# Decoder megakernel, last feed-forward: accumulators copied out by ScalarE, roots in pieces, norm on ScalarE

## The chip, the cores and the metric

The kernel runs on one core of a Trainium2 chip, in one launch. The metric is the device time of the launch in microseconds (us). The run before has three timed executions and, apart from them, one profiled execution, from which all durations below come.

## The reference

Two decoder layers run over x (4 batches, 512 positions, 512 features), each as attention, cross attention and feed-forward, each with a residual and a layer norm behind it. The change concerns the last of the six parts alone:

```python
def _L1_ffn_ref(x, gate_up_packed, gate_up_scales, down_packed, down_scales):
    ...
    gate_up = jnp.einsum('bsh,oh->bso', x, w_gu)      # weights from 4-bit codes, 11 blocks of 128 rows
    gate, up = (gate_up[..., :I], gate_up[..., I:])
    h = jax.nn.silu(gate) * up
    y = jnp.einsum('bsi,hi->bsh', h, w_down)
    rms = jnp.sqrt(jnp.mean(y * y, axis=-1, keepdims=True) + EPS)   # EPS = 1e-06
    return y / rms
...
x = _layernorm(x + _L1_ffn_ref(x, ...), axis=-1)      # mean and variance over 512, eps 1e-05
return x
```

## The kernel before

**Batches and lanes.** The six parts are called A to F, and a batch of a part is a task (F0 to F3 are the last feed-forward). Each task is a Python generator that issues instructions and yields; two tasks are live at a time and take turns. A task that yields "next" lets the following one start. So when F0 has issued its last up-projection it yields "next", and its ending is issued in turn with the beginning of F1. A `Pipe` delays a step by a number of ticks (`F_SCALED` 1, `F_ACT` 5, `F_PAIR` 3, `F_DOWN` 9). From what is issued, a scheduler settles the order on each engine; each engine then works its own queue strictly in that order and waits on semaphores.

**One batch of F.** x is loaded as four tiles of 128 positions (names `x`), transposed (`fx`) and split into a high and a low part. For each of 11 blocks i, for u = 0 (gate) and 1 (up), and for each of four groups g of 128 features, two matmuls fill a PSUM bank named `fg` (L1080). `scaled` takes the bank out: for g = 0 ScalarE multiplies by the group's scale (L1038); else VectorE multiplies and adds to the sum in SBUF (L1044, one scalar_tensor_tensor); for u = 0, g = 3 ScalarE makes a second tile (L1041) that GpSimd adds (L1048). Then Silu on ScalarE (L1052), gate times up on VectorE (L1056), the high part as a cast on ScalarE (`fhh`, L1061) and the low part on GpSimd (`fhl`, L1062). `down` issues three matmuls for each of the four position tiles t into four accumulators `facc` (L1071), which hold four of the eight PSUM banks through all 11 blocks. In all a batch has 176 matmuls into `fg` and 132 into `facc`.

**The ending of a batch.** It follows the "next": x is loaded again; ScalarE squares each accumulator and sums the row (L1090); VectorE makes the mean square (L1093) and its inverse root with an integer seed and three Newton steps (`rsqrt`, L158 to L163, 128x4 values); L1097 on VectorE adds accumulator times root to x, reading the accumulator in PSUM, and `ln_stats` takes bn_stats and bn_aggr of the sum (L168, L169). `finish` runs a second root (L177, then L158 to L163), the norm on VectorE (L186) and the stores from the SP queue (L189). The accumulators' banks are free when L1097 has read them.

Of the kernel before, what the change touches and what calls it, by code (L numbers as in the profile page):

```python
# [14 lines left out]
I32 = mybir.dt.int32  # L15
U8 = mybir.dt.uint8
AF = mybir.ActivationFunctionType
ALU = mybir.AluOpType
# [4 lines left out]
P = 128  # L23
NT = 4
MAGIC = 12582912.0
RSQRT_SEED = float(0x5F3759DF)
# [38 lines left out]
class Net:  # L65
# [88 lines left out]
    def rsqrt(self, ve, s):  # L154

        nc = self.nc
        sh, y, t = s[:, 0:4], s[:, 4:8], s[:, 8:12]
        nc.vector.tensor_scalar(sh.bitcast(I32), ve.bitcast(I32), 1, None, ALU.logical_shift_right)  # L158
        nc.vector.tensor_scalar(y.bitcast(I32), sh.bitcast(I32), -1.0, RSQRT_SEED, ALU.mult, ALU.add)
        for _ in range(3):  # L160
            nc.vector.tensor_tensor(t, y, y, ALU.mult)
            nc.vector.scalar_tensor_tensor(t, t, -0.5, ve, ALU.mult, ALU.mult)
            nc.vector.scalar_tensor_tensor(y, t, 1.5, y, ALU.add, ALU.mult)  # L163
        return y

    def ln_stats(self, y, i, ln):
        nc = self.nc
        nc.vector.bn_stats(ln[:, 8:14], y)  # L168
        nc.vector.bn_aggr(ln[:, 2 * i : 2 * i + 2], ln[:, 8:14])  # L169
# [852 lines left out]
    def l1_ffn(self, b):  # L1022
        nc = self.nc
        pipe = Pipe()
        x = self.load_x(5, b)
        yield
        yield
        xT = []
        yield from self.feature_major(pipe, x, "fx", xT)
        yield from pipe.drain()  # L1030
        acc, y, hs = [], {}, {}

        def scaled(i, u, g, ps):

            s = self.gs[:, (i * 2 + u) * 4 + g : (i * 2 + u) * 4 + g + 1]
            if g == 0:
                y[u] = self.t("fg")
                nc.scalar.activation(y[u], ps, AF.Copy, scale=s)  # L1038
            elif g == 3 and u == 0:
                y2 = self.t("fg2")  # L1040
                nc.scalar.activation(y2, ps, AF.Copy, scale=s)  # L1041
                y[u, 2] = y2
            else:
                nc.vector.scalar_tensor_tensor(y[u], ps, s, y[u], ALU.mult, ALU.add)  # L1044
            if g == 3:
                o = y.pop(u)
                if (u, 2) in y:
                    nc.gpsimd.tensor_tensor(o, o, y.pop((u, 2)), ALU.add)  # L1048
                pipe.later(F_ACT, *((up, i, o) if u else (gate, o)))

        def gate(o):
            nc.scalar.activation(o, o, AF.Silu)  # L1052
            y["gate"] = o

        def up(i, o):
            nc.vector.tensor_tensor(o, o, y.pop("gate"), ALU.mult)  # L1056
            pipe.later(F_PAIR, pair, i, o)

        def pair(i, o):
            hi, lo = self.t("fhh", F32R), self.t("fhl", F32R)  # L1060
            nc.scalar.copy(hi, o)  # L1061
            nc.gpsimd.tensor_tensor(lo, o, hi.bitcast(F32), ALU.subtract)  # L1062
            for t in range(NT):
                pipe.later(F_DOWN + 2 * t, down, i, t, (hi, lo))

        def down(i, t, h):
            if len(acc) <= t:
                acc.append(self.pb("facc"))
            c = slice(t * P, (t + 1) * P)
            for n, (l, r) in enumerate(((0, 0), (0, 1), (1, 0))):  # L1070
                nc.tensor.matmul(acc[t], h[l][:, c], self.dn[i][r], start=i == 0 and n == 0, stop=i == 10 and n == 2)  # L1071

        for i in range(11):
            self.need("F", lambda: len(self.dn) > min(10, i + 1))
            for u in range(2):
                for g in range(4):
                    pipe.tick()
                    ps = self.pa("fg")
                    for n in range(2):
                        nc.tensor.matmul(ps, self.gu[i, u][:, g * P : (g + 1) * P], xT[g][n], start=n == 0, stop=n == 1)  # L1080
                    pipe.later(F_SCALED, scaled, i, u, g, ps)
                    yield
        yield "next"
        x = self.load_x(5, b)
        yield from pipe.drain()
        fm = self.s("fm", 24, 2)
        ss, ve = fm[:, 0:4], fm[:, 4:8]
        for i in range(NT):
            sq = self.t("fsq")
            nc.scalar.activation(sq, acc[i], AF.Square, accum_out=ss[:, i : i + 1])  # L1090
            if i % 2:
                yield
        nc.vector.tensor_scalar(ve, ss, 1.0 / 512.0, 1e-6, ALU.mult, ALU.add)  # L1093
        r = self.rsqrt(ve, fm[:, 8:20])
        ln = self.ln_tile()
        for i in range(NT):
            nc.vector.scalar_tensor_tensor(x[i], acc[i], r[:, i : i + 1], x[i], ALU.mult, ALU.add)  # L1097
            self.ln_stats(x[i], i, ln)
            if i % 2:
                yield  # L1100
        self.finish(pipe, x, ln, 5, b)
        yield from pipe.drain()

    def need(self, key, ready):

# [121 lines left out]
```

## Time and profile before

| | us |
|---|---|
| median of three runs | 1662.6 (1662.27 to 1663.54) |
| profiled execution | 1662.88 |
| its span, first to last instruction | 1660.9 |
| mean granted TensorE clock | 0.978 of full |

| engine | busy us | share of the span |
|---|---|---|
| TensorE matmul (PE) | 1549.7 | 93% |
| VectorE (DVE) | 1267.4 | 76% |
| ScalarE (ACT) | 1007.5 | 61% |
| GpSimd (POOL) | 667.4 | 40% |

| instruction of F | count | mean ns |
|---|---|---|
| L1044 VectorE scaled sum | 220 | 745 |
| L1038 ScalarE scaled first sum | 88 | 686 |
| L1090 ScalarE square of an accumulator, and its readback | 16 | 594, 201 |
| L1097 VectorE update of x | 16 | 738 |
| L1048 GpSimd add | 44 | 1387 |
| L1062 GpSimd low part | 44 | 1317 |

In rows of the profile "L1044 DVE" is line 1044 on VectorE, "fg<-fg,gs,fg" the tiles written and read, and "[1.92 <-DVE fg L1044]" an idle time of the engine before that instruction, in us, and what ended it. Busy time of matmuls counts overlapping instructions once; a busy TensorE can still be slowed, which the granted clock shows.

### The profile page before, as it was taken

How to read it: one execution, taken by the hardware profiler on the slowest of the kernel's cores; microseconds unless marked ns; L12 is line 12 of the kernel's file. 1: busy time of each engine (PE TensorE's matmuls, PEld its weight loads, DVE VectorE, ACT ScalarE, POOL GpSimd, SP SyncE). 2: the span in 40 equal slices, each digit the busy share in tenths (PEclk: the TensorE clock that was granted, in tenths of full speed). 3: DMA queues.
4: the chain of work that ended last, by engine and by line, in shares of the span. 5: the costliest groups of instructions: out<-in, count | busy, mean ns of one | idle time of the engine just before them, and what ended most of it. 6: DMA issues, size and time to landing. Idle time of an engine off the chain costs nothing.

```text
span 1660.9 us, 25661 instructions
## 1 busy us (share of the span) xinstructions
PE 1549.7 (93%) x8246; PEld 1110.3 (67%) x8246; DVE 1267.4 (76%) x2796; ACT 1007.5 (61%) x2149; POOL 667.4 (40%) x672
## 2 busy tenths in 40 slices
PE   7999999999999899899999999999988889999995
PEld 5888775444544674466777767777667766786874
DVE  6386688999976678876565675756879999979795
ACT  5333326888778867786696865968533445444542
POOL 5663653555535203420435332343323344333332
PEclk9999998999999999999999999999998999999998
DMA  7043343455114634763433323333444532021000
GB/s 243 28 146 121 127 133 118 144 165 184 58 71 146 193 114 138 205 188 98 127 77 77 77 64 109 83 77 77 153 152 123 189 106 63 9 69 47 5 26 25
DMA packets 103237, 180.77 MB, mean 109 GB/s; under 512 B 16560, under 2 KB 18608, under 8 KB 103104
## 3 DMA queue, kind: packets, MB, share of 16 engines
q1 hardware_dynamic: 98976, 170.69, 32.8%
q0 software_dynamic: 4128, 8.46, 2.1%
q8 instruction: 65, 1.06, 0.3%
q14 instruction: 68, 0.56, 0.1%
HBM read 111.98 MB, written 41.94 MB: 93 GB/s over the span
## 4 chain that ended last, share of the span: by engine, by line
PE 54%; DVE 23%; ACT 9%; DMA 7%; issue 4%; POOL 2%; SPq 1%; DVEq 0%; ACTq 0%; POOLq 0%
PE fg L1080 7%; PE facc L1071 6%; DVE bsm L413 3%; PE dT L857 2%; ACT de L847 2%; PE pu L626 2%; PE pg L624 2%; DVE x L186 2%; DMA z<-had_scratch 2%; DVE fg L1044 2%; PE dn L678 2%; PE dq L146 2%; PE dq L147 2%; PE dq L148 2%; PE do L877 2%
## 5 line engine op out<-in xcount | busy, mean ns | idle before, releaser
L1044 DVE SCALAR_TENSOR_TENSOR fg<-fg,gs,fg 128x512 f32<-128x512 f32 x220 | 162.4, 745 | 36.8 <-PE fg L1080 17.5
L1080 PE MATMUL fg<-fxh,gu 128*128 128x512 f32 x352 | 144.2, 410 | 7.5 <-DVE fg L1044 4.6
L847 ACT ACTIVATE de<-de,dm 128x128 f32<-128x128 f32 (+3 forms) x256 | 143.0, 563 | 13.4 <-DVE dm L846 12.4
L846 DVE CUSTOM_DVE_ANT_0 de<-ds,negm,thr 128x128 f32<-128x128 f32 (+3 forms) x256 | 126.5, 546 | 31.0 <-PE ds L835 27.9
L421 POOL TENSOR_SCALAR be<-be,bsm 128x512 f32<-128x512 f32 x128 | 95.7, 760 | 120.5 <-DVE bsm L419 70.4
L1080 PE MATMUL fg<-fxl,gu 128*128 128x512 f32 x352 | 139.2, 395 | 0.0
L603 POOL TENSOR_TENSOR hl<-g,hh 128x512 fp32r<-128x512 f32 x64 | 84.2, 1323 | 114.6 <-ACT hh L602 93.4
L1048 POOL TENSOR_TENSOR fg<-fg,fg 128x512 f32<-128x512 f32 x44 | 61.0, 1387 | 128.4 <-ACT fg L1041 69.5
L415 ACT ACTIVATE be<-bs,bsm 128x512 f32<-128x512 f32 x128 | 87.5, 690 | 39.3 <-DVE bsm L413 32.3
L777 POOL TENSOR_TENSOR dql<-dqf,dqh 128x512 fp32r<-128x512 f32 x32 | 41.4, 1295 | 154.5 <-ACT dqh L776 120.8
L857 PE MATMUL dT<-ident,de 128*128 128x128 f32 x640 | 89.9, 278 | 7.9 <-ACT de L847 5.9
L1080 PEld LDWEIGHTS fg<-fxh,gu 128*128 128x128 f32 x352 | 67.3, 191 | 38.1 <-DVE fg L1044 14.2
L857 PEld LDWEIGHTS dT<-ident,de 128*128 128x128 f32 x640 | 71.7, 141 | 25.6 <-ACT de L847 14.4
L1038 ACT ACTIVATE fg<-fg,gs 128x512 f32<-128x512 f32 x88 | 60.4, 686 | 39.1 <-PE fg L1080 38.6
L413 DVE TENSOR_REDUCE bsm<-bs 128x1 f32<-128x512 f32 x128 | 84.0, 674 | 0.1
L692 PE MATMUL had<-had,z 128*128 128x128 f32 x512 | 75.0, 293 | 9.5 <-DMA z<-had_scratch 9.3
L692 PEld LDWEIGHTS had<-had,z 128*128 128x128 f32 x512 | 68.9, 203 | 17.1 <-issue 6.4
L1071 PE MATMUL facc<-p4h,fhh 128*128 128x512 f32 x176 | 71.7, 409 | 8.9 <-DVE fg L1044 6.2
L437 PE MATMUL bo<-bpT,cT 128*64 128x512 f32 x256 | 75.4, 625 | 3.5 <-ACT bpT L428 1.5
L199 PEld LDWEIGHTS bT<-ident,be 128*128 128x128 f32 x512 | 55.1, 141 | 34.4 <-issue 12.9
L199 PE MATMUL bT<-ident,be 128*128 128x128 f32 x512 | 73.7, 283 | 3.9 <-POOL be L421 1.4
L1041 ACT ACTIVATE fg<-fg,gs 128x512 f32<-128x512 f32 x44 | 30.2, 687 | 75.1 <-PE fg L1080 75.1
(330 smaller groups left out, 4715.8 us busy)
## 6 DMA issues: line engine op xcount, KB each, us to landing
x<-x SPq DMA_DIRECT2D x176, 256.0 KB, 3.1
had_scratch<-hw SPq DMA_DIRECT2D x64, 256.0 KB, 2.0
z<-had_scratch SPq DMA_DIRECT2D x64, 256.0 KB, 6.6
stk<-dqh SPq DMA_DIRECT2D x192, 64.0 KB, 2.1
tw<-in_wg_t SPq DMA_DIRECT2D x32, 256.0 KB, 4.1
tw<-in_wu_t SPq DMA_DIRECT2D x32, 256.0 KB, 3.5
tw<-in_wd_t SPq DMA_DIRECT2D x32, 256.0 KB, 2.7
p<-in_gu_p SPq DMA_DIRECT2D x22, 256.0 KB, 2.7
```

The source lines that it names most:

```text
L199: self.nc.tensor.transpose(pt[:, i * P : (i + 1) * P], srcs[i][:, j * P : (j + 1) * P], self.ident)
L413: nc.vector.tensor_reduce(sm[:, h : h + 1], ps, AX.X, ALU.max, negate=True)
L415: nc.scalar.activation(e, ps, AF.Exp, bias=sm[:, h : h + 1], accum_out=sm[:, 2 + h : 3 + h])
L421: nc.gpsimd.tensor_scalar(es[h][i], es[h][i], sm[:, 4 + h : 5 + h], 1.0, ALU.mult, ALU.mult)
L603: nc.gpsimd.tensor_tensor(lo, g, hi.bitcast(F32), ALU.subtract)
L692: nc.tensor.matmul(ps[:, c * P : (c + 1) * P], z[g * 4 + c][:, i * P : (i + 1) * P], self.had16, start=True, stop=True)
L846: nc.vector.tensor_tensor_reduce(es[i], ps, self.negm[:, 384 - P * i :], -1.0, self.thr[:, i : i + 1], ALU.add, ALU.min, n4[:, i : i + 1])
L847: nc.scalar.activation(es[i], es[i], AF.Exp, bias=n4[:, i : i + 1], scale=-1.0, accum_out=den[:, hh * 4 + i : hh * 4 + i + 1])
L857: nc.tensor.transpose(pt[:, o + (i - j) * P : o + (i - j + 1) * P], es[i][:, j * P : (j + 1) * P], self.ident)
L1044: nc.vector.scalar_tensor_tensor(y[u], ps, s, y[u], ALU.mult, ALU.add)
L1071: nc.tensor.matmul(acc[t], h[l][:, c], self.dn[i][r], start=i == 0 and n == 0, stop=i == 10 and n == 2)
L1080: nc.tensor.matmul(ps, self.gu[i, u][:, g * P : (g + 1) * P], xT[g][n], start=n == 0, stop=n == 1)
```

## The change

At the end of a batch of F, four ScalarE copies take the accumulators from PSUM to SBUF tiles `fy`, each as its accumulator closes; squares and the update of x read `fy`. The root is issued in pieces by a generator, `rsqrt_spread`, which yields before each Newton step; `issue_after(self.summed.ins)` puts each piece on VectorE's queue behind the latest scaled sum issued so far, of whichever batch. The update of x also writes its row sum (`accum_out`). GpSimd makes the negative mean from it (128x1), ScalarE squares x less its mean and sums the row, VectorE makes the second root, GpSimd mean times root (128x4), and ScalarE applies the norm and issues the store from its own queue. bn_stats, bn_aggr, VectorE's norm and SP's stores of this part are gone. The order on all engines is unchanged up to the first ending of F.

```diff
             else:
-                nc.vector.scalar_tensor_tensor(y[u], ps, s, y[u], ALU.mult, ALU.add)
+                self.summed = nc.vector.scalar_tensor_tensor(y[u], ps, s, y[u], ALU.mult, ALU.add)
...
+    def newton(self, ve, y, t):
+        nc = self.nc
+        nc.vector.tensor_tensor(t, y, y, ALU.mult)
+        nc.vector.scalar_tensor_tensor(t, t, -0.5, ve, ALU.mult, ALU.mult)
+        nc.vector.scalar_tensor_tensor(y, t, 1.5, y, ALU.add, ALU.mult)
+
+    def rsqrt_spread(self, ve, s):
+        nc = self.nc
+        sh, y, t = s[:, 0:4], s[:, 4:8], s[:, 8:12]
+        with self.tc.issue_after(self.summed.ins):
+            nc.vector.tensor_scalar(sh.bitcast(I32), ve.bitcast(I32), 1, None, ALU.logical_shift_right)
+            nc.vector.tensor_scalar(y.bitcast(I32), sh.bitcast(I32), -1.0, RSQRT_SEED, ALU.mult, ALU.add)
+        for _ in range(3):
+            yield
+            with self.tc.issue_after(self.summed.ins):
+                self.newton(ve, y, t)
...
+        ys = [self.o("fy") for i in range(NT)]
+        for i in range(NT):
+            nc.scalar.copy(ys[i], acc[i])
         for i in range(NT):
             sq = self.t("fsq")
-            nc.scalar.activation(sq, acc[i], AF.Square, accum_out=ss[:, i : i + 1])
+            nc.scalar.activation(sq, ys[i], AF.Square, accum_out=ss[:, i : i + 1])
             if i % 2:
                 yield
         nc.vector.tensor_scalar(ve, ss, 1.0 / 512.0, 1e-6, ALU.mult, ALU.add)
-        r = self.rsqrt(ve, fm[:, 8:20])
+        yield from self.rsqrt_spread(ve, fm[:, 8:20])
+        r = fm[:, 12:16]
         ln = self.ln_tile()
-        for i in range(NT):
-            nc.vector.scalar_tensor_tensor(x[i], acc[i], r[:, i : i + 1], x[i], ALU.mult, ALU.add)
-            self.ln_stats(x[i], i, ln)
+        tot, nmean, sq, nr = (ln[:, 4 * n : 4 * n + 4] for n in range(4))
+        for i in range(NT):
+            nc.vector.scalar_tensor_tensor(x[i], ys[i], r[:, i : i + 1], x[i], ALU.mult, ALU.add, accum_out=tot[:, i : i + 1])
+            nc.gpsimd.tensor_scalar(nmean[:, i : i + 1], tot[:, i : i + 1], -1.0 / 512.0, 1.0, ALU.mult, ALU.mult)
+            t = self.t("fsq")
+            nc.scalar.activation(t, x[i], AF.Square, bias=nmean[:, i : i + 1], accum_out=sq[:, i : i + 1])
             if i % 2:
                 yield
-        self.finish(pipe, x, ln, 5, b)
-        yield from pipe.drain()
+        v2 = ln[:, 16:20]
+        nc.vector.tensor_scalar(v2, sq, 1.0 / 512.0, 1e-5, ALU.mult, ALU.add)
+        yield from self.rsqrt_spread(v2, ln[:, 20:32])
+        r2 = ln[:, 24:28]
+        nc.gpsimd.tensor_tensor(nr, nmean, r2, ALU.mult)
+        yield
+        for i in range(NT):
+            nc.scalar.activation(x[i], x[i], AF.Identity, bias=nr[:, i : i + 1], scale=r2[:, i : i + 1])
+            nc.scalar.dma_start(self.xd[6][b, i * P : (i + 1) * P, :], x[i])
+            yield
```

More of the change, by code (lines that the diff above doesn't have):

```diff
@@ L160, in rsqrt @@
         for _ in range(3):
-            nc.vector.tensor_tensor(t, y, y, ALU.mult)
-            nc.vector.scalar_tensor_tensor(t, t, -0.5, ve, ALU.mult, ALU.mult)
-            nc.vector.scalar_tensor_tensor(y, t, 1.5, y, ALU.add, ALU.mult)
-        return y
+            self.newton(ve, y, t)
+        return y
+    def newton(self, ve, y, t):
[12 more added lines that the diff above has]
+            with self.tc.issue_after(self.summed.ins):
+                self.newton(ve, y, t)
     def ln_stats(self, y, i, ln):
```

## The prediction

> **What bounds the kernel now.** I read the busy shares first, then the chain of waits over the last stage, then busy time by stretch, then the instructions of one hand-over and of the tail.
>
> ```profile
> PE 1549.7 (93%) x8246; PEld 1110.3 (67%) x8246; DVE 1267.4 (76%) x2796; ACT 1007.5 (61%) x2149; POOL 667.4 (40%) x672
> ```
>
> TensorE leads, but only the stretches say what that is worth here. In the chain of waits three equal places mark the period of one batch in the last feed-forward, and one row gives its matmul pace:
>
> ```profile
> 1453.62 1.19 PE fg L1080 x4
> ...
> 1532.14 1.20 PE fg L1080 x4
> ...
> 1610.65 1.20 PE fg L1080 x4
> ...
> 1635.20 6.13 PE facc L1071 x27
> ```
>
> A period is 78.5 us. A matmul costs 6.13 / 27 = 0.227 us, so a batch's 176 + 132 matmuls need 69.9 us, and 16 transposes (0.87 us for eight in the same chain) 1.7: 71.6. So 6.9 us are lost per period. The table of stretches says where (us, then busy PE, PEld, DVE, ACT, POOL, then the granted clock):
>
> ```profile
> 1454.00:1480.00 26.00, 26.00 (x119) 21.50 (x118) 19.61 (x28) 12.30 (x21) 10.45 (x9) 1.00 0.18 59
> 1494.00:1532.00 38.00, 35.09 (x140) 26.16 (x138) 36.24 (x71) 18.85 (x36) 14.53 (x11) 0.96 0.03 11
> ```
>
> Between hand-overs TensorE is full and VectorE at 75%; during the hand-over (old batch's norm beside the new batch's first sums) VectorE is at 95% and TensorE waits. The timeline of that place:
>
> ```profile
> 1498.22 0.16 DVE L1093 TENSOR_SCALAR fm<-fm 128x4 f32<-128x4 f32 x1
> 1498.47 1.29 POOL L1048 TENSOR_TENSOR fg<-fg,fg 128x512 f32<-128x512 f32 x1 [3.10 <-DVE fm L1093]
> 1498.62 1.17 DVE L159 TENSOR_SCALAR fm<-fm 128x4 int32<-128x4 int32 x1
> ...
> 1501.93 0.50 PE L1071 MATMUL facc<-p4h,fhh 128*128 128x512 f32 x1 [1.92 <-DVE fg L1044]
> ...
> 1502.83 0.63 PE L1071 MATMUL facc<-p4h,fhh 128*128 128x512 f32 x1
> ...
> 1528.10 1.67 POOL L1048 TENSOR_TENSOR fg<-fg,fg 128x512 f32<-128x512 f32 x1 [2.29 <-ACT fg L1038]
> ```
>
> A root step of 0.16 us takes 1.17 where it meets a GpSimd add, and ends with it. One idle of 1.92 us is followed by matmuls of 0.63 us at 0.43 us pace: the granted clock reads 0.50 from 1502.5 to 1505.9. The last row (1.67 instead of 1.29) is GpSimd waiting for a VectorE product that reads SBUF twice, and VectorE's next operation then waited for it: they take turns. The tail:
>
> ```profile
> 1643.89 0.19 ACT L1090 ACTIVATION_READ_ACCUMULATOR fsq<-facc 128x1 f32 x1
> 1644.12 0.17 DVE L1093 TENSOR_SCALAR fm<-fm 128x4 f32<-128x4 f32 x1 [7.14 <-ACT fsq L1090]
> ...
> 1646.50 1.41 DVE L1097 SCALAR_TENSOR_TENSOR x<-facc,fm,x 128x512 f32<-128x512 f32 x2
> ...
> 1655.59 1.79 SPq L189 DMA_DIRECT2D out_dram<-x  x4
> ```
>
> Nothing covers this one: squares, root, update and statistics, root, norm, store, to the span's end at 1660.9.
>
> **The change, on the clock of the hand-over at 1494.** The order of instructions in the changed program is known; I follow it with these durations. Starts advance by 0.57 on ScalarE for a scaled sum or square, 0.5 for a copy; on VectorE by 0.66 for a scaled sum, 0.84 if it needs the one before, 0.2 for a root step that needs the one before.
>
> *Copies.* Four ScalarE copies of some 0.59 us (rows for casts out of PSUM) start at 1490.7, 1492.3, 1494.4 and 1495.5, as each accumulator closes, on an engine at 50%. They free four banks some 14 us earlier than L1097 does, and push the next batch's first scaled sum from 1495.92 to 1496.6 and the last square's readback to 1498.4: the root begins at 1498.8, not 1498.22. Price alone: 0.6.
>
> *First root.* The five leading steps meet one GpSimd add (1499.1 to 1500.4), as now; then Newton steps alternate with four new sums. It ends at 1504.6, where before it ended at 1506.8: 2.2 gained.
>
> *What VectorE loses.* Four bn_stats (0.69), four aggregates (0.18) and four norms (2.88 together) leave it: 6.4 us a batch. That is the cover the change counts on.
>
> *What the change queues.* The four x updates stand back to back, directly followed by the second root's start, which waits for ScalarE's fourth square, which waits for GpSimd's fourth mean. Seven root steps follow before the next new sum. On ScalarE the four squares stand ahead of the next cast fhh and the next three evacuations, so it idles too. An update: 0.67 (spacing of the L1097 pair, 1.41 less 0.74), plus an accumulator readback of 0.08 (L846's row, 83 ns): 0.75. It now reads SBUF twice, so GpSimd's means (0.29, from L650's 287 ns) take turns with it: I add two turns, 0.6; the bounds are zero and three. Updates run 1504.6 to 1508.2, the last two means to 1508.8, the last square with readback to 1509.6. The cast starts at 1509.4, GpSimd's split at 1510.1, which blocks a root step until 1511.4; the first new sum starts at 1512.3. The one before it started at 1502.6: VectorE serves TensorE nothing for 9.7 us.
>
> *TensorE.* It has matmuls until 1504.1. Then three new accumulators and five unread sums hold all eight banks, and its next matmul wants the cast: idle to 1510.1, 6.0 us against 1.92 now. Then about seven matmuls at 0.43 instead of 0.227 (3.4 us of half clock, as after the idle of 1.92): 1.4. A second such stretch would cost up to 1.6 more, counted in the range only. Waits for single banks add 0.9 before 1504 (three, each for the sum just made) and 1.2 from 1513 to 1517, when VectorE's sums come 0.84 apart or meet GpSimd. From 1517.9 a run of 17 accumulator matmuls that need no bank (3.9 us) covers the norms and store issues that hold ScalarE from 1517.1 to 1520.9; without that cover those 3.8 us would be idle too. I leave 0.2 for what sticks out. Sum: 0.9 + 6.0 + 1.4 + 1.2 + 0.2 = 9.7 lost. Against 6.9, each hand-over loses 2.8 more; three make +8.3. Without turns block and idle are 1.0 shorter: 8.7 each and +5.4.
>
> [...] L409, the nearest row with two f32 SBUF inputs and no accumulator, has a minimum of 0.673 us, the 0.67 that I take. [...]
>
> *Tail.* All of it is on the path. Four copies and waiting squares put the root's start at 1646.2, not 1644.12: +2.1. Its 2.38 us are unchanged. From first update to second root: four times 0.75, two turns 0.6, last means 0.6, square with readback and hand-overs 0.9, makes 5.1 against 6.13 now (1646.50 to 1652.63): -1.0. Then a GpSimd product (0.3 with its wait 0.4): two norms of 0.58, two store issues, two norms, two issues, all on ScalarE. An issue costs 0.37 (L189's median, on SP; none on ScalarE is shown: bounds 0.05 and 0.5). That is 0.4 + 2.3 + 1.5 = 4.2 from root to last issue, against 1655.01 to 1657.38 = 2.4: +1.8. Tail +2.9. Moving 16 stores off SP is worth nothing: its waits there are for norms.
>
> *Sum.* 1660.9 + 8.3 + 2.9 = 1672.1 span. The profiled execution took 1662.88, 1.98 outside its span; the median of the three runs is 0.28 below. So 1672.1 + 1.98 - 0.28 = 1673.8, call it 1674.
>
> **Rivals.** *Faster (0.08):* the early copies give TensorE banks that outlast the block. For it: four banks 14 us earlier, VectorE 6.4 us lighter. Against: the bank count at 1504. It decides if the idle stays under about 2.2 us: the 2.8 more per hand-over and a third of the tail (1.0) make 3.8, and 6.0 less 3.8 is 2.2. If idle and slow clock vanish, some 3 us are lost per hand-over, 3.9 fewer than now: 3 x -3.9 + 2.9 = -8.8, so 1653.8.
> *Only the tail (0.10):* the early gain pays for the idle and hand-overs still lose 6.9: 1665.5.
> *Dear updates and a longer slow clock (0.12):* an update of 0.97 (L409's maximum) plus 0.19 (ScalarE's readback, L847's row) is 1.16, 1.6 more for four; the tail makes it four such groups, +6.6; a second slow stretch three times, +4.8: 1685.
> *As worked out (0.70):* 1674, within 1668.5 and 1680.5. Below: no turns (-2.9 and, with the means, -0.9 in the tail), issues of 0.05 (-1.3). Above: a third turn in four groups (+1.2), issues of 0.5 (+0.5), the second slow stretch alone (+4.8).
>
> **Numbers.** Some 0.2% (3.3 us) is what a measurement tells from no change. Faster takes 0.07 of the first rival; same takes its weak outcomes (0.01) and nearly all of the second (0.09); the rest, 0.83, is slower. The range, 1664.5 to 1683, leaves out the first rival, the low edge of the second and about half of the third, under 0.2 in all.
>
> **What would show it.** Right: in the hand-over VectorE has four updates, then a wait for ScalarE's square; TensorE one idle of 5 to 6 us ended by the cast; granted clock 0.5 after it; period near 81.3; time from the last matmul's end to the span's end near 20.4 us, now 17.5. Wrong: idle under 2.2 us there, a period below 78.5, or updates above 1.1 us.

## The result, and the profile after

The changed kernel takes 1677.6 us (median of six runs, 1671.0 to 1679.8), the kernel before beside it 1664.0 (1662.3 to 1668.2): a ratio of 1.0072, 95% interval 1.0051 to 1.0094. By the ratio it is slower by some 12 us. Its profiled execution was the quickest of the six (1671.02, span 1669.3).

The shares on the page of the changed kernel show the relief that was intended, 21 us on VectorE, and no gain from it:

```profile
PE 1550.4 (93%) x8246; PEld 1111.0 (67%) x8246; DVE 1246.4 (75%) x2764; ACT 1039.8 (62%) x2213; POOL 674.1 (40%) x692
```

VectorE's first step of the first root (L1113) stands once in each hand-over, so the distance of two of them is a period. Both lines are the changed kernel's:

```profile
1498.73 0.16 DVE L1113 TENSOR_SCALAR fm<-fm 128x4 f32<-128x4 f32 x1
1580.80 0.16 DVE L1113 TENSOR_SCALAR fm<-fm 128x4 f32<-128x4 f32 x1
```

That is 82.07 us against 78.50 (1498.22 to 1576.72): 3.6 more per hand-over. Less the 71.6 of matmuls, 10.5 are lost where 6.9 were. The stretch of the hand-over, in the columns of the prediction's table:

```profile
1494.00:1532.00 38.00, 32.19 (x123) 24.06 (x122) 29.20 (x62) 22.77 (x45) 13.74 (x14) 0.87 0.17 56
```

VectorE is down from 36.24 to 29.20 us busy, and so is TensorE, from 35.09 to 32.19; the granted clock fell from 0.96 to 0.87. None of them is busy throughout. The timeline of the changed kernel shows on whom they wait:

```profile
1504.71 0.75 DVE L1120 SCALAR_TENSOR_TENSOR x<-fy,fm,x 128x512 f32<-128x512 f32 x1
1505.38 0.08 DVE L1120 DVE_READ_ACCUMULATOR x<-fy,fm,x 128x1 f32 x1
...
1505.56 2.21 POOL L1121 TENSOR_SCALAR ln<-ln 128x1 f32<-128x1 f32 x4 [5.16 <-DVE x L1120]
...
1506.22 0.72 ACT L1123 ACTIVATE fsq<-x,ln 128x512 f32<-128x512 f32 x1 [5.16 <-POOL ln L1121]
...
1509.05 0.60 ACT L1077 CAST fhh<-fg 128x512 fp32r<-128x512 f32 x1
1509.18 0.17 DVE L1127 TENSOR_SCALAR ln<-ln 128x4 f32<-128x4 f32 x1 [1.69 <-ACT fsq L1123]
...
1509.71 0.80 PE L1087 MATMUL facc<-p4h,fhh 128*128 128x512 f32 x1 [5.28 <-ACT fhh L1077]
...
1511.74 0.75 DVE L1060 SCALAR_TENSOR_TENSOR fg<-fg,gs,fg 128x512 f32<-128x512 f32 x1
```

Read the brackets from the bottom up. TensorE idles 5.28 us for ScalarE's cast. The cast's input is the product L1072, which ended at 1504.2; but in ScalarE's queue four squares stand ahead of it, and ScalarE idles 5.16 us until GpSimd's first mean, which waits for VectorE's first update. VectorE in turn waits 1.69 us for the last square. Between 1502.7 and 1511.7 VectorE starts no sum for the new batch. A cast whose input had been ready for 4.8 us stood behind work of the old batch: for 2.0 us of that ScalarE idled (to 1506.22), for 2.8 it worked on the four squares.

### The profile page after: what moved, and what is told of

It reads as the page before. It is cut to its first block, busy times and chain, and to the rows that moved or that the text cites. A ratio compares the mean times of both kernels' runs of the same rounds, so it can differ in the third digit from the quotient of the medians.

```text
span 1669.3 us, 25728 instructions
## 1 busy us (share of the span) xinstructions
PE 1550.4 (93%) x8246; PEld 1111.0 (67%) x8246; DVE 1246.4 (75%) x2764; ACT 1039.8 (62%) x2213; POOL 674.1 (40%) x692
## 4 chain that ended last, share of the span: by engine, by line
PE 58%; DVE 21%; ACT 9%; DMA 5%; issue 4%; POOL 2%; SPq 1%; ACTq 0%; DVEq 0%; POOLq 0%
PE fg L1096 8%; PE facc L1087 6%; PE dT L873 2%; PE pu L642 2%; DVE bsm L429 2%; ACT de L863 2%; PE pg L640 2%; PE dn L694 2%; PE bo L453 2%; PE dq L146 2%; PE bT L215 2%; PE dq L147 2%; PE dq L148 2%; PE do L893 2%; PE had L708 2%
## 5 line engine op out<-in xcount | busy, mean ns | idle before, releaser
L1054 ACT ACTIVATE fg<-fg,gs 128x512 f32<-128x512 f32 x88 | 60.4, 687 | 34.1 <-PE fg L1096 32.4
L1096 PEld LDWEIGHTS fg<-fxl,gu 128*128 128x128 f32 x352 | 67.9, 193 | 12.7
```

## The experiments

Two numbers are read from every profile. The **period** is the distance of two starts of the first root, as above. **From first root** is the time from the first such start to the span's end; it leaves out all that comes ahead of the change. That part ends at 1416.6 to 1424.2 us in these profiles, which is why single times say less than these two. Both, and the clock, come from one profiled execution of each kernel; a stretch of half clock more or less moves a period by 0.7 to 1.3 us (kernels 7, 8 and 11), so a period difference of about 1 us between two kernels can be that alone.

| kernel | ratio to before, 95% interval | periods, us | from first root, us | longest idle of TensorE in a hand-over, us | half clock per hand-over, us |
|---|---|---|---|---|---|
| before | 1 | 78.6, 78.5 | 241.2 | 1.9 | 3.4 |
| changed | 1.0072 (1.0051 to 1.0094) | 82.2, 82.1 | 252.7 | 5.3 | 10.2 |
| 1 stores from SP | 1.0075 (1.0061 to 1.0090) | 82.7, 83.2 | 254.7 | 5.3 | 10.2, 6.8, 6.8 |
| 2 copies alone | 1.0042 (1.0026 to 1.0058) | 79.6, 80.0 | 246.2 | 1.4 | 0 |
| 3 more turns | 1.0069 (1.0053 to 1.0084) | 81.7, 82.7 | 252.3 | 3.9 | 6.8 |
| 4 bn_stats kept | 1.0015 (1.0003 to 1.0026) | 78.3, 78.3 | 243.1 | 1.1 | 0 |
| 5 ScalarE's norm alone | 1.0006 (0.9993 to 1.0019) | 79.1, 78.4 | 241.8 | 1.9 | 3.4 |
| 6 statistics alone | 1.0024 (1.0011 to 1.0037) | 80.2, 80.2 | 244.4 | 2.3 | 3.4 |
| 7 updates apart | 1.0066 (1.0045 to 1.0086) | 81.0, 81.1 | 249.9 | 2.7 | 3.4 |
| 8 same, other tail | 1.0046 (1.0029 to 1.0064) | 82.3, 82.1 | 249.4 | 2.7 | 6.8 |
| 9 same, cast first | 1.0125 (1.0110 to 1.0140) | 84.8, 84.8 | 258.6 | 3.0 | 0, 0, 6.8 |
| 10 cast first | 1.0080 (1.0065 to 1.0095) | 82.0, 82.0 | 252.4 | 2.1 | 6.8 |
| 11 tail alone | 0.9991 (0.9979 to 1.0003) | 78.4, 77.6 | 237.1 | 1.9 | 3.4, 0, 0 |
| 12 parts put together | 0.9995 (0.9979 to 1.0010) | 78.6, 78.7 | 238.9 | 1.2 | 0 |

My theory at the start was the one of the prediction: VectorE's row of updates and second root, with ScalarE's squares ahead of the cast, starves TensorE. The rivals were that the copies cost the time, that the stores on ScalarE's queue do, and that the added work itself does.

**1. Stores from SP.**

```diff
-            nc.scalar.dma_start(self.xd[6][b, i * P : (i + 1) * P, :], x[i])
+            nc.sync.dma_start(self.xd[6][b, i * P : (i + 1) * P, :], x[i])
```

> The changed kernel with one edit: the last part's stores are issued from SP's queue instead of ScalarE's. My theory (the block: four updates, the wait for GpSimd's means and ScalarE's squares, the second root, all ahead of the new batch's sums) says that the stores play no part in the hand-over: the period of a batch stays at 82.0 us, TensorE's idle before the cast stays near 5.3 us, and the granted clock stays at half for some 10 us after it. Only the tail gains: two pairs of issues leave ScalarE (last norm 0.7 us earlier), so 0 to 2 us less than the changed kernel, some 1676. The rival that ScalarE's queue is held by the stores says: period back toward 79 to 80 us, 6 to 9 us less in all, some 1669.

The period grew by 0.6 and 1.1 us instead of staying. The stores are not at fault; without them the four norms stand in one row of 2.9 us on ScalarE, and the new batch's scaled sum behind them is late. The waits of TensorE in this kernel (total us, times, longest) have a line that the changed kernel lacks:

```profile
PE facc L1087 <- ACT fhh L1077: 15.8, 3, 5.3
PE fg L1096 <- ACT fg L1054: 3.3, 3, 1.6
```

**2. The copies alone**, on the kernel before:

```diff
+        ys = [self.o("fy") for i in range(NT)]
+        for i in range(NT):
+            nc.scalar.copy(ys[i], acc[i])
...
-            nc.scalar.activation(sq, acc[i], AF.Square, accum_out=ss[:, i : i + 1])
+            nc.scalar.activation(sq, ys[i], AF.Square, accum_out=ss[:, i : i + 1])
...
-            nc.vector.scalar_tensor_tensor(x[i], acc[i], r[:, i : i + 1], x[i], ALU.mult, ALU.add)
+            nc.vector.scalar_tensor_tensor(x[i], ys[i], r[:, i : i + 1], x[i], ALU.mult, ALU.add)
```

> The kernel before with the early ScalarE copies alone: squares and the update read the copies; first root in one lump, bn_stats and bn_aggr, VectorE's norm and SP's stores as before. On VectorE the updates are then again followed by new sums and there is no block. My theory says that the copies themselves cost a hand-over nothing or gain, since four banks come free earlier: TensorE's idle there at most 1.9 us as before, half clock at most 3.4 us, period 75.5 to 78.5 us (before: 78.5, changed kernel: 82.0); the tail loses 2 us by its later root; in all 1657 to 1666, at or below the kernel before. The rival that the copies, or the half microsecond by which they push the new batch's first sums, cause the loss says: period near 82 and 1675 or more.

The longest idle fell to 1.4 us and the half clock vanished, which lies within what I had expected, and yet the period rose by 1.0 to 1.5 us: TensorE now has 21 short waits in the three hand-overs (10.1 us on VectorE's sums, 4.5 on ScalarE's). The copies do cost something in a hand-over, which I had excluded, but less than half of the 3.6. The tail lost the 2.0 that were expected (from the first accumulator's reader to the end 21.5 us against 19.5).

**3. More turns for the new batch:** in the loop of updates two turns after each update instead of one after every second, and four more behind the loop.

```diff
-            if i % 2:
-                yield
+            yield
+            yield
+        for _ in range(4):
+            yield
```

> The changed kernel with more turns handed to the new batch: two after each update and four ahead of the second root. The same instructions all run; on VectorE the order is now four updates, two sums, second root's start, then sums and root steps alternating, and on ScalarE the cast of the next block stands after two of the four squares and not after all of them. My theory says: TensorE's idle falls from 5.3 us to 2 to 3.5, the half clock from 10.2 us to 3.4 to 6.8, the period from 82.0 to 77 to 80 us, so 6 to 15 us less than the changed kernel; the tail stays. The rival that the work itself costs (updates that read SBUF twice, small GpSimd means, four more ScalarE squares a batch) says: the same work runs, so the period stays within 0.5 us of 82.0 and the time within 3 us of the changed kernel.

The half clock fell to 6.8 us as expected and the idle to 3.9, less far than the 2 to 3.5 expected; the period did not fall (81.7 and 82.7), and the time, by its ratio that of the changed kernel, is the one named for the rival. What left the long idle came back in shorter waits over the next 30 us.

**4. Statistics as before**, all else as changed:

```diff
-            nc.vector.scalar_tensor_tensor(x[i], ys[i], r[:, i : i + 1], x[i], ALU.mult, ALU.add, accum_out=tot[:, i : i + 1])
-            nc.gpsimd.tensor_scalar(nmean[:, i : i + 1], tot[:, i : i + 1], -1.0 / 512.0, 1.0, ALU.mult, ALU.mult)
-            t = self.t("fsq")
-            nc.scalar.activation(t, x[i], AF.Square, bias=nmean[:, i : i + 1], accum_out=sq[:, i : i + 1])
+            nc.vector.scalar_tensor_tensor(x[i], ys[i], r[:, i : i + 1], x[i], ALU.mult, ALU.add)
+            self.ln_stats(x[i], i, ln)
```

> The changed kernel with its statistics as before: bn_stats and bn_aggr on VectorE in place of the row sums, GpSimd's four means and ScalarE's four squares; copies, pieces of the root, ScalarE's norm and ScalarE's stores stay as changed. VectorE's order is then: updates, bn_stats and aggregates with new sums between them, no wait for ScalarE; the changed kernel's chain from VectorE over GpSimd and ScalarE back to VectorE is gone. My theory says: period 75 to 78.5 us; tail longer than before by 2 (later root) and 1.8 (norm and issues on ScalarE); in all 1655 to 1667. The rival that copies, pieced root, ScalarE's norm or its stores cause the loss says: period above 80 and 1672 or more.

78.3 us: the whole 3.6 that the change had added to a hand-over is gone, though VectorE has 3.5 us a batch more to do. Copies, pieces of the root, ScalarE's norm and its stores together cost a hand-over nothing; what is left of the ratio is the tail. This is the run that names the part. The idle of 5.3 is gone from TensorE's waits:

```profile
PE fg L1096 <- DVE fg L1060: 9.8, 15, 1.1
PE fg L1096 <- ACT fg L1054: 1.0, 3, 0.3
```

**5. ScalarE's norm alone**, on the kernel before, for the first three batches (the last batch keeps VectorE's norm):

```diff
+        nc.gpsimd.tensor_tensor(nr, nmean, r2, ALU.mult)
...
+            nc.scalar.activation(x[i], x[i], AF.Identity, bias=nr[:, i : i + 1], scale=r2[:, i : i + 1])
+            nc.scalar.dma_start(self.xd[6][b, i * P : (i + 1) * P, :], x[i])
```

> The kernel before with one part of the change alone: for the first three batches of the last feed-forward ScalarE applies the norm and issues the stores, GpSimd makes the negative mean and the bias; the last batch keeps VectorE's norm and SP's stores. Copies, statistics and the root in a lump stay as before. The run with the copies alone lost 1.6 us more per period than the run that had ScalarE's norm besides, so I expect 1.3 us per hand-over (the time that TensorE waits 32 us after the root's start, when VectorE makes four norms): period 76.9 to 78.0, time 1658 to 1662. If ScalarE's part in the end of a batch is what slows the changed kernel, the period is above 79 and the time above 1664.

No gain where 1.3 us a hand-over were expected. TensorE no longer waits for VectorE's norms, but 0.3 to 1.1 us for a cast that now stands behind ScalarE's four norms and four stores (1531.89 to 1535.74 in its timeline): the price moved from one queue to the other.

**6. The statistics alone**, on the kernel before (updates with row sum, GpSimd's mean and ScalarE's square as in the change; norm on VectorE from the negative mean, stores from SP):

```diff
+            nc.vector.scalar_tensor_tensor(x[i], acc[i], r[:, i : i + 1], x[i], ALU.mult, ALU.add, accum_out=tot[:, i : i + 1])
+            nc.gpsimd.tensor_scalar(nmean[:, i : i + 1], tot[:, i : i + 1], -1.0 / 512.0, 1.0, ALU.mult, ALU.mult)
+            t = self.t("fsq")
+            nc.scalar.activation(t, x[i], AF.Square, bias=nmean[:, i : i + 1], accum_out=sq[:, i : i + 1])
...
+            nc.vector.tensor_scalar(x[i], x[i], nmean[:, i : i + 1], r2[:, i : i + 1], ALU.add, ALU.mult)
```

> The kernel before with another part of the change alone: row sums from the update, GpSimd's negative means, ScalarE's squares of x less its mean; no copies, roots in one lump, norm on VectorE, stores from SP. In VectorE's queue the first root, four updates, the wait for ScalarE's square, and six steps of the second root now stand in a row with no sum of the new batch between them, though VectorE has 3.5 us less to do. My theory, that this row of instructions is what starves TensorE, says: idle of 5 us or more in each hand-over, half clock behind it, period 81 to 85 us, time 1668 to 1682. The rival that copies, pieces of the root, ScalarE's norm or its stores are at fault says: period 78.5 or below, time 1662 or below, because VectorE is lighter.

Period 80.2, not 81 to 85: my theory gave too much, the rival (78.5 or less) too little. A VectorE lighter by 4.3 us a batch (1250.2 us busy in all against 1267.4) came with a hand-over 1.7 us longer. TensorE waits 2.3 us, now for the first update (which frees an accumulator), and 1.4 to 1.8 for a sum behind the second root.

**7. Updates apart:** as changed, but each update is held behind the latest sum, with six turns after each.

```diff
+            with self.tc.issue_after(self.summed.ins):
-            nc.vector.scalar_tensor_tensor(x[i], ys[i], r[:, i : i + 1], x[i], ALU.mult, ALU.add, accum_out=tot[:, i : i + 1])
+                nc.vector.scalar_tensor_tensor(x[i], ys[i], r[:, i : i + 1], x[i], ALU.mult, ALU.add, accum_out=tot[:, i : i + 1])
...
-            if i % 2:
+            for _ in range(6):
                 yield
```

> The changed kernel with all of its instructions, but each update is held behind the latest scaled sum and six turns are handed to the new batch after each update. On VectorE the order is then update, 2 sums, update, 4 sums, update, 4 sums and products, update, 3, start of the second root; on ScalarE a cast stands behind at most one square. My theory says that with the block dissolved the gain that the lighter VectorE should have brought appears: TensorE's longest idle under 2 us, half clock at most 3.4 us a hand-over, loss per hand-over 4.5 to 6.5 us, period 76 to 78 us, time 1655 to 1664. The rival that the work itself costs (two-input updates, small GpSimd operations, four more squares, copies) says: loss and period as in the changed kernel, 82 us, time above 1672.

The theory's number fell: 81.0 and 81.1 us, and a median of 1674.1; the rival's numbers are nearer. VectorE's row of updates was dissolved, and TensorE still waited for the cast, as the timeline of this kernel shows:

```profile
1504.92 0.72 ACT L1123 ACTIVATE fsq<-x,ln 128x512 f32<-128x512 f32 x1 [4.72 <-POOL ln L1121]
...
1505.64 0.60 ACT L1077 CAST fhh<-fg 128x512 fp32r<-128x512 f32 x1
...
1506.29 0.50 PE L1087 MATMUL facc<-p4h,fhh 128*128 128x512 f32 x1 [2.73 <-ACT fhh L1077]
```

One square stands ahead of the cast, and ScalarE sits idle for 4.72 us with the cast's input ready since 1503.3. With one, two and four squares ahead of the cast (kernels 7, 3 and the changed one) the idle is 2.7, 3.9 and 5.3 us: 0.7 to 1.1 more per square, and squares stand 0.71 apart. So ScalarE's queue, which the prediction had named only beside VectorE's, carries the long idle, by waits and by the squares' own work.

**8. The same with another tail:** for the last batch no copies; two norms on VectorE with stores from SP, two on ScalarE.

> The dissolved kernel with another ending of the last batch, which nothing covers: no copies there (squares and updates read the accumulators in PSUM), and the last norm is split, two tiles on VectorE with stores from SP and two on ScalarE with stores from its own queue. Hand-overs as in the dissolved kernel. The root of the last batch should start 2.0 us earlier after its first accumulator, and root to last issue take 2.0 to 2.5 us instead of 4.2: 3.5 to 4.5 us less than the dissolved kernel. Under my theory 1651 to 1660 in all, below the kernel before; under the rival 1668 or more.

The tail did what was expected: from the first accumulator's reader to the end 17.5 us against 21.0. The time, 1669.8, is again the one named for the rival. The hand-overs did not get better, and by chance show a price: order and idle are those of kernel 7, but the half clock lasted 6.8 us and not 3.4, and the period is 1.0 to 1.3 us longer.

**9 and 10. The cast first.** In both the squares of x are held behind the latest cast. Kernel 9 adds it to kernel 8 (three turns ahead of the first update, four after each); kernel 10 to the changed kernel (four turns ahead of the updates), so that VectorE's row of updates stays.

```diff
+            self.cast = nc.scalar.copy(hi, o)
...
+            with self.tc.issue_after(self.cast.ins):
+                nc.scalar.activation(t, x[i], AF.Square, bias=nmean[:, i : i + 1], accum_out=sq[:, i : i + 1])
```

> Both blocks opened: the dissolved kernel with its better ending of the last batch, and now the squares of x are held behind the latest cast, with three turns ahead of the first update and four after each. On ScalarE the next cast and two scaled sums stand ahead of the first square; on VectorE updates alternate with sums. If the two queues' order is the cause, TensorE's longest idle is under 1.5 us, no half clock follows, the loss per hand-over is 4.5 to 6.5 us, the period 76 to 78 us, time 1653 to 1660, below the kernel before. If the changed work itself costs the time, the loss stays above 9 us and the period above 81 us, whatever the order, time 1666 or more.

> The dissolved kernel kept one thing: on ScalarE a square that waits for update, root and GpSimd's mean still stood ahead of the next block's cast, and TensorE's idle before that cast was 2.7 us with one square ahead, 3.9 with two, 5.3 with four. So my theory now has two blocks, VectorE's and ScalarE's. This run keeps the first and takes away the second: the changed kernel, but the squares of x are held behind the cast, and four turns are given to the new batch ahead of the updates. ScalarE's order is cast, scaled sum, four squares; VectorE still has four updates, the second root's start and six steps in a row without a sum. If ScalarE's block alone costs the time, TensorE's wait for the cast vanishes, no idle is over 1.5 us, the loss per hand-over is 6 to 7.5 us and the period 77.5 to 79 us, time 1662 to 1668. If VectorE's block does it, the cast comes early and TensorE still stops, for a VectorE sum, 3 to 5 us, and the period is 80 to 82.5 us, time 1670 to 1678. I hold the second the likelier by a little: eight banks last no longer than some 4 us.

Kernel 10 has the period and time of its second case, but not its mechanism, a stop of 3 to 5 us for a VectorE sum: the wait for the cast fell to 1.4 us, others of 2.1 (a tile that ScalarE scales behind the four squares) and 1.2 (VectorE's sums) took its place, and the period stayed at 82.0. Kernel 9, in which I had held both blocks to be open, is the slowest of all. Its timeline:

```profile
1514.84 0.75 DVE L1124 SCALAR_TENSOR_TENSOR x<-fy,fm,x 128x512 f32<-128x512 f32 x1
1515.69 0.19 POOL L1125 TENSOR_SCALAR ln<-ln 128x1 f32<-128x1 f32 x1 [4.97 <-DVE x L1124]
1515.92 0.72 ACT L1128 ACTIVATE fsq<-x,ln 128x512 f32<-128x512 f32 x1 [5.78 <-POOL ln L1125]
1516.64 0.67 ACT L1054 ACTIVATE fg<-fg,gs 128x512 f32<-128x512 f32 x1
...
1517.34 1.60 DVE L1060 SCALAR_TENSOR_TENSOR fg<-fg,gs,fg 128x512 f32<-128x512 f32 x2 [1.74 <-ACT fg L1054]
1518.86 0.74 DVE L1124 SCALAR_TENSOR_TENSOR x<-fy,fm,x 128x512 f32<-128x512 f32 x1
```

Follow the brackets: VectorE's sums wait for ScalarE's scaled first sum (L1054), which stands behind a square, which waits for GpSimd's mean, which waits for an update, which now stands behind sums. Four updates among the sums make four such rounds, where the row of updates made one. Both engines idle, at once. So the theory that the row of updates is the block, and that it only needs opening, falls. What I read from the traces in its place: the statistics tie VectorE's, GpSimd's and ScalarE's queues into a chain, and wherever a link stands in a queue worked strictly in order, the new batch's work behind it waits for all links ahead. Five orders of the hand-over's same instructions (the changed kernel, 3, 7, 9 and 10) lost 9.4 to 13.2 us each; with chain and work of the statistics taken out (4) it is 6.7.

The rival that the changed work itself costs, whatever the order, is not excluded by this: kernels 3, 7 and 9 came out at or near the numbers named for it. Against it as the whole cause speak the engines that idle in these traces and the spread with the order, 9.4 to 13.2 us; for a part of it speaks the changed kernel's cast, which the squares' work held for 2.8 of its 4.8 us. No run had the same work without the chain, so how much each of the two costs is not shown.

**11. The tail alone**, on the kernel before: the last batch has the row-sum statistics, with its norm on VectorE and its stores on SP.

> The kernel before with another ending for the last batch alone, where no matmul is left to cover anything: row sums from the update, GpSimd's means, ScalarE's squares in place of bn_stats and bn_aggr; squares of y straight from PSUM, norm on VectorE, stores from SP. The three hand-overs are untouched: period 78.5 us. From first update to second root 4.0 to 4.5 us instead of 6.1, so 1.7 to 2.1 us less than the kernel before, some 1660; the ratio near 0.999. The rival that the row-sum chain costs more than bn_stats wherever it stands says 0 to 2 us more.

Where no matmul is left, the same chain pays: from first update (1641.37) to second root (1645.41) 4.04 us against 6.13, the tail 17.5 against 19.5. The ratio, 0.9991, is 1.5 us in the expected direction, but its interval reaches over 1. Two of its hand-overs had no half clock after the same idle of 1.9 us; the period that begins with one of them was 77.6.

**12. The parts that did not hurt, put together**, kernel 4's hand-overs and kernel 11's tail, with the second root's Newton steps on GpSimd:

```diff
+            nc.gpsimd.tensor_tensor(t, r2, r2, ALU.mult)
+            nc.gpsimd.tensor_tensor(t, t, v2, ALU.mult)
+            nc.gpsimd.tensor_scalar(t, t, -0.5, 1.5, ALU.mult, ALU.add)
+            nc.gpsimd.tensor_tensor(r2, r2, t, ALU.mult)
...
+            with self.tc.issue_after(self.cast.ins):
+                nc.scalar.activation(x[i], x[i], AF.Identity, bias=nr[:, i : i + 1], scale=r2[:, i : i + 1])
```

> The parts that did not hurt, put together: for the first three batches early copies, first root in pieces, bn_stats and bn_aggr on VectorE, ScalarE's norm and stores (the run with bn_stats lost 6.65 us per hand-over, with VectorE busy without a gap for 30 us and its short root steps held up to 1.2 us each by GpSimd's adds); new here, the nine Newton steps of the second root are twelve small operations on GpSimd, and the norms stand behind the latest cast and twenty turns. For the last batch no copies, and the row-sum ending of the run that changed the tail alone. VectorE sheds nine steps and two or three of the holds, some 4 us in a hand-over: loss 4.5 to 6.5 us, period 76.2 to 78.2 us; the tail 2 us shorter than before; 1654 to 1660 in all, below both kernels. If GpSimd's twelve operations hold up its add and so Silu and the next cast, a new wait for the cast appears, loss 7 to 9 us, time 1661 to 1668.

It beats the changed kernel and cannot be told from the kernel before (0.9995). The tail is 17.5 us, as in kernel 11. The hand-overs lose 7.0 where 4.5 to 6.5 were expected, which with the time is the second case named before the run. Most of TensorE's waits there are for VectorE's sums (1.2 us the longest); some 1 us a hand-over (0.4 for the cast, 0.6 for GpSimd's low part after it) is the old pattern in a new place:

```profile
1529.11 1.52 ACT L1159 ACTIVATE x<-x,ln 128x512 f32<-128x512 f32 x2 [2.81 <-POOL ln L1154]
1529.96 1.04 ACTq L1160 DMA_DIRECT2D out_dram<-x  x2
1531.04 0.62 ACT L1077 CAST fhh<-fg 128x512 fp32r<-128x512 f32 x1 [0.41 <-ACT x L1159]
```

ScalarE idles for GpSimd's root, with a cast behind two norms and two stores whose input (a product begun at 1526.10) was long there.

## Why the prediction was right, and where it was not

The median, 1677.6, lies in the range, and the ratio on 1662.6 gives 1674.6 against 1674. Step by step, for one hand-over and then the tail:

| step | predicted us | measured us |
|---|---|---|
| waits for banks ahead of the idle | 0.9 | 1.2 |
| idle until the cast | 6.0 | 5.5 |
| half clock behind it | 1.4 | 2.6 |
| waits for banks behind it, and the rest | 1.4 | 1.0 |
| lost per hand-over | 9.7 | 10.3 |
| tail: later root | +2.1 | +2.0 |
| first update to second root | -1.0 | -1.7 |
| second root to last issue | +1.8 | +1.8 |
| last issue to the end | 0 | -0.5 |
| tail in all | +2.9 | +1.6 |

(Lost time is the sum over one period of each matmul's distance to the next less 0.227. The tail runs from the first reader of an accumulator, to 21.04 us from 19.48.)

- **The mechanism** was the predicted one: updates, the wait for GpSimd and ScalarE, TensorE's single long idle ended by the cast. The first root's start came at 1498.73 against 1498.8, the first update at 1504.71 against 1504.6, the cast at 1509.05 against 1509.4. The rival *faster* needed an idle under 2.2 us and falls with 5.3; *only the tail* needed periods of 78.5.
- **The half clock was the mis-sized term.** I took one stretch of 3.4 us because one had followed the idle of 1.92; three followed, 10.24 us in a row from 1505.8, of which matmuls met 6.4: 13 of them at 0.43 instead of 0.227, so 2.6 lost. Every stretch in these profiles is one, two or three times 3.41 us; equal idles of 5.3 us brought 10.2 and 6.8 (kernel 1), and an idle of 1.9 brought one stretch in seven of nine hand-overs (kernels before, 5 and 11). What more the runs show of it is in the last section. The rival *dear updates and a longer slow clock* was right in its second half alone: the slow clock came longer, the updates stayed at 0.75.
- **The turns between GpSimd's means and two-input updates** I had added to VectorE: 0.6. VectorE paid nothing (spacing 0.67); GpSimd paid, 2.21 us for four means. So the idle was 0.5 shorter than predicted.
- **An update** took 0.75 us with a readback of 0.08, as predicted, and updates follow each other at 0.67.
- **The tail** was 1.3 too dear: the turns (0.6) and means that I put there did not come, and the landing was 0.5 quicker (2.97 against 3.52).
- **Part of the closeness is luck.** In a hand-over the half clock and the first waits were 1.5 us too small, the idle and the later waits 0.9 too large; three times the remaining 0.6 is largely offset by the tail. In the sum itself three times 2.8 is 8.4, not 8.3, and the low edge adds up to 1668.9, not 1668.5; neither changes the outcome.
- **The reason** was half right. I held VectorE's 9.7 us without a sum and ScalarE's squares ahead of the cast to be one block in that order. Opening either alone (7, 10), or both (9), gave back 1 us, nothing, or less than nothing. The part to blame is shown by run 4: the statistics, which run from VectorE over GpSimd and ScalarE back. How much of it is their chain of waits and how much their work, no run separates. Runs 2 and 6 also show that the parts don't add up: copies alone cost 1.0 to 1.5 us a hand-over, statistics alone 1.7, together with the rest 3.6, and all without the statistics -0.2. Why the copies alone cost time, and with ScalarE's norm do not, stays open. A chain without GpSimd's mean between update and square was not tried.

## What to carry to other kernels

Before work is moved from a busy engine to idle ones, count the waits that it adds between queues that run strictly in order, and what stands behind each waiting instruction: here 7 us less of VectorE's work in a hand-over came with 3.6 us more of TensorE's time lost. Opening a row of instructions that blocks did not help here: its links stayed tied to the work that they were put between, and in kernel 9 every link became a block of its own. In the profiles the same chain gained 2 us at the end of the kernel, where nothing stands behind it, so hand-overs and tails want different code.

## What the runs showed of the hardware

- The half clock (0.50 granted) came in stretches of 3.41 us, none to three of them, and the same idle did not always bring the same number: 2.7 us brought one in kernel 7 and two in kernel 8, 1.9 us one or none in kernel 11, 3.0 us none in two hand-overs of kernel 9. One stretch more cost a period 0.7 us (kernel 11) to 1.3 (kernels 7 and 8).
- In each profile the starts of the half clock in these hand-overs lie whole multiples of 3.413 us apart (the kernel before drops at 1424.09 and 1502.60 us, 23 multiples). In the 3.41 us ahead of each of the 29 starts that the 14 profiles show there, TensorE's rows left 1.48 us (the changed kernel's third) or more idle. In kernel 7's first hand-over 2.69 us of idle lay in the 3.41 us ahead of the start, and one stretch followed; in kernel 8's 2.04 lay ahead of it and 0.81 in the 3.41 us behind it, and two followed. Kernel 11 has one start, in its first hand-over. Counted from there in steps of 3.413 us, one step holds 1.84 us of the idle of 1.9 in its second hand-over, and two steps hold 1.1 and 1.0 us idle in its third: no half clock followed either. What decides between none, one and two is not shown by these runs.
- A GpSimd operation on 128x1 took 0.19 us alone (kernel 7) and up to 0.63 beside the changed kernel's updates on VectorE from two SBUF inputs, while these kept their spacing of 0.67. Beside updates that read one input from PSUM (last batch of kernels 11 and 12) it took 0.19 to 0.20.
- Stores issued by ScalarE are not free to it: two norms and the issue of their two stores held its queue for 1.92 us (1531.89 to 1533.81 in kernel 5), where the norms alone took 1.51.
